# Weights' loads behind the squares' exchange, look-ups in front of the transposition, values' products in the squares' order

## The chip, the cores and the metric

The kernel runs on one core of one Trainium2 chip. The metric is the device time of one execution in microseconds; lower is better. A core has a matrix engine (TensorE, PE in the profile, with its weight loads as PEld), a vector engine (VectorE, DVE), a scalar engine (ScalarE, ACT), GpSimd (POOL) and SyncE (SP), which here only issues transfers. Each engine works through its own instructions in order; semaphores tie them together. Sixteen DMA engines move the data, and the transfers that one engine issues stand in one queue.

## The reference

Two transformer layers on `x` of 8 sequences x 512 tokens x 256 features, all in float32. Layer 0 is a rotating recurrence and a mixture of 16 experts. Layer 1 is causal attention with 16 heads of 128 and a feed-forward layer whose three weight matrices are looked up in a table of 16 values. The change lies in layer 1:

```python
# attention, W_K, W_Q, W_V: (16, 128, 256)
scores = jnp.einsum('biph,biqh->biqp', k, q)
masked = scores * mask - 1e10 * (1.0 - mask)
attn = softmax(masked / sqrt(128), axis=-1)
z = jnp.einsum('biqp,biph->biqh', attn, v)
out = jnp.einsum('df,bqf->bqd', W_O, z_flat)
# feed-forward, lut: (16,), *_idx: integers 0..15
h = silu(x @ lut[gate_idx].T) * (x @ lut[up_idx].T)
x = x + h @ lut[down_idx].T
```

## The kernel before

The span has four parts: layer 0 up to about 570 us, the attention of layer 1 from 570 to 2046 us, then the feed-forward layer to the end at 2277 us. The change is in the attention.

**The turns.** The attention is one Python loop over 8 sequences x 8 pairs of heads x 2 heads (`for p in range(ALL)`, `for e in range(2)`): 128 passes, called turns here. A turn is counted from its first score product, and numbered 0 to 15 in its sequence; sequences are numbered 0 to 7. Even turns have e = 0, odd turns e = 1. The order in which PE, DVE and SP are given their instructions is the order in which the loop calls them (`tc.manual_schedule(engines={ENG.PE, ENG.DVE, ENG.SP})`); ACT and POOL are ordered by a scheduler.

**One head passes through three turns.** In its first, `scores(0..3)` makes the four causal score tiles of 128 queries (PE, L1070), masks them and takes the extreme value (DVE, L1074), and exponentiates with the sum (ACT, L1085). `normalized` scales the tiles by the reciprocal sum (DVE L1093, ACT L1099) into `slots`, a tile of 10 blocks in 32-wide pieces. In the second turn the probabilities are transposed without TensorE: `squares_turned` transposes each 32 x 32 square (DVE, L1108) and writes the squares to memory with four transfers (SP, L1111); `exchanged` reads them back as `pT` in the order of the squares (SP, L1116), which completes the transposition of the whole. In the third turn `weigh` multiplies the values by `pT` (PE, L1140, four products into the PSUM bank `pz`) and copies the result to `z` (ACT, L1147). So a turn works on three heads: scores of one, exchange of the one before (`front`), values' products of the one before that (`rear`). `pT` and `pz` have one buffer each, `slots` two. The last two heads are turned by TensorE instead (`turned`, L1118).

**Projections.** Queries, keys, values and the output are made by a scheme of seven products in place of eight (`Sevens`, L239 to 264): four products and the sums on DVE in `first`, three products in `second`. Even turns make queries and the first half of keys for the next pair (`nxt`); odd turns finish the keys (`nxt.second(1)`) and make half of the values of the next group (`ahead`). The PSUM banks `pa` and `pb` are single, so the products of `ahead.second` wait until DVE has read `pb` (L253).

**Weights.** When a `second` has used a weight tile, `following_weights` loads the one for a later pair at once (`load_weights`, L739 to 745: 128 KB from the input and, once the five sums of the tile are kept in memory, 320 KB from there). The tiles `w0`, `w1` have two buffers, `wv` and `wo` one. The load waits for the last product that reads the old tile, and SP can issue nothing else while it waits.

**Outputs.** Every four heads, `Outputs` makes the products with the output weights (L1194) in four pieces, one in each turn at the call `one_out()`; a quarter's last piece also asks for the next `wo`. With the last quarter of a sequence GpSimd adds the kept sums (`summed`, L1210), and two more pieces turn the result with four transposes by TensorE each (L1229). In turns 2, 3 and 4 of a sequence a second `one_out()` stands in front of `scores(2)` where enough pieces are left.

**Look-ups.** The table look-ups for the feed-forward layer (`lookups`, L947 to 953) are spread over the attention: a generator, of which each turn from sequence 1 on takes one step on DVE, behind `weigh`.

Of the kernel before, what the change touches and what calls it, by code (L numbers as in the profile page):

```python
# [10 lines left out]
F32 = mybir.dt.float32  # L11
I32 = mybir.dt.int32
AF = mybir.ActivationFunctionType
# [102 lines left out]
def two_layers(ctx: ExitStack, tc: tile.TileContext, a: dict, out: bass.AP):  # L116
# [848 lines left out]
    with tc.tile_pool(name="big", bufs=2, side="right") as big, tc.tile_pool(  # L965
# [31 lines left out]
            return [pool.tile([P, T], F32, tag=tag, name=tag).rearrange("p (k t) -> p k t", k=2) for _ in range(2)]  # L997

        incomplete = []

        def following_weights(n, part):
            if part is not None:
                w, complete = load_weights(n, part, part not in seen_parts[n])
                weights[n].append(w)
                seen_parts[n].add(part)
                if complete:
                    incomplete.append((n, complete))
# [49 lines left out]
        class Head:  # L1057
# [29 lines left out]
            def normalized(self, *tiles):  # L1087

                if 0 in tiles:
                    self.slots = ap2.tile([P, NQ, NS, SQ], F32, name="slots")  # L1090
                w = self.slots
                rd = self.rd[:, tiles[0] : tiles[-1] + 1]
                nc.vector.reciprocal(rd, self.den[:, tiles[0] : tiles[-1] + 1])  # L1093
                for i in tiles:

                    for j in range(0, i + 1, 2):
                        n = min(i + 1 - j, 2)
                        at, step = SLOT[j, i], SLOT[j + n - 1, i] - SLOT[j, i]
                        nc.scalar.activation(  # L1099
                            w[:, :, at : at + step + 1 : max(step, 1), :].rearrange("p q j k -> p j q k"),  # L1100
                            self.pr[i][:, j * P : (j + n) * P].rearrange("p (j q k) -> p j q k", q=NQ, k=SQ),
                            AF.Copy,
                            scale=self.rd[:, i : i + 1],
                        )

            def squares_turned(self):

# [27 lines left out]

            def weigh(self):

                pz = pzp.tile([P, T], F32, tag="pz", name="pz")
                for j in range(NT):
                    nc.tensor.matmul(  # L1140
                        pz[:, j * P :].rearrange("p (i q k) -> p i q k", q=NQ, k=SQ),
                        self.v(j),
                        self.of_keys(j),
                        start=(j == 0),
                        stop=(j == NT - 1),
                    )
                nc.scalar.copy(self.z, pz)  # L1147


        late = []  # L1150
# [1 line left out]
        def in_time():  # L1152
            while late:
                late.pop(0)()
# [82 lines left out]
        def outputs(quarter, eng=nc.gpsimd):  # L1237

            quarter.combined(eng)
            last = quarter.q == NGRP - 1  # L1240
            n = quarter.b * NGRP + quarter.q + 1

            def end(*banks):
                quarter.products(3, *banks)
                if n < NB * NGRP:
                    following_weights("o", n % NGRP)
                if last:
                    in_time()
                    quarter.summed(eng)

            pieces = [lambda *banks, i=i: quarter.products(i, *banks) for i in range(3)] + [end]
            if last:
                pieces += [lambda *banks, h=h: quarter.turned(h, *banks) for h in range(2)]
            return pieces

        def one_out():
# [30 lines left out]
        with tc.manual_schedule(engines={ENG.PE, ENG.DVE, ENG.SP}):  # L1287
            seqs[0].xn = first_xn
            for c in range(NC):
                seqs[0].turned(c)  # L1290
            seqs[0].combined()
            following_weights("o", 0)

            pairs[0].first(0)
            pairs[0].first(1, lambda: other_banks(psc, "sc"))
            pairs[0].second(0, 2)
            groups[0].first(0)
            pairs[0].second(1, 2)
            groups[0].first(1, lambda: other_banks(ptp, "pt"))
            for s in range(2):  # L1300
                groups[0].second(s, s or None)

            front = rear = None
            for p in range(ALL):
                b, pair = divmod(p, NPAIR)
                nxt = pairs[p + 1] if p + 1 < ALL else None
                after = (p + 3) % NPAIR if p + 3 < ALL else None
                ahead = groups[p // 2 + 1] if p // 2 + 1 < len(groups) else None
                if pair % 2 == 0:
                    z = big.tile([P, VG, T], F32, tag="big", name="zT")  # L1310
                for e in range(2):
                    head = Head(
                        *(pairs[p].of_head(n, e) for n in range(2)),
                        lambda j, g=groups[p // 2], h=2 * (p % 2) + e: g.of_head(j, h),
                        z[:, 2 * (pair % 2) + e, :],
                        e,
                        p < ALL - 1,
                    )
                    in_time()
                    if front and not front.by_slots:  # L1320
                        one_out()
                        rear.weigh()
                        front.turned()
                        rear = None
                    head.scores(0)
                    head.scores(1)
                    if front and front.by_slots:
                        front.squares_turned()
                    one_out()
                    if nxt:  # L1330
                        nxt.second(1, after) if e else nxt.first(0)
                    if rear:
                        rear.weigh()
                    in_time()
                    while rows_to_gather and rows_to_gather[0][0] <= 2 * p + e:
                        gather(*rows_to_gather.pop(0)[1])
                    if b:
                        next(look, None)
                    if rear and e and pair % 2 == 0:
                        quarter = Outputs(*divmod(p // 2 - 1, NGRP), done, kept)  # L1340
                        tiles_out += outputs(quarter)
                    if not e and nxt:
                        nxt.second(0, after)
                    if e and ahead:
                        ahead.first(p % 2)
                    if head.by_slots:
                        head.normalized(0, 1)

                    slot = (2 * pair + e) % VG
                    if slot != 1 and len(tiles_out) > -slot % VG + 1:  # L1350
                        one_out()
                    head.scores(2)
                    head.scores(3)
                    if front and front.by_slots:
                        front.exchanged()
                    in_time()
                    if e and ahead:
                        last_half = p % 2 == 1
                        ahead.second(p % 2, (p // 2 + 2) % NGRP if last_half and p // 2 + 2 < len(groups) else None)
                    if not e and nxt:  # L1360
                        nxt.first(1)
                    if head.by_slots:
                        head.normalized(2)
                        head.normalized(3)

                    complete_weights(*(("v",), (0, 1, "o"))[e])
                    front, rear = head, front

                    if pair == 3 and e == 0 and b + 1 in together:
                        taken = row_stats(*together[b + 1])  # L1370
                        if len(together[b + 1]) > 1:
                            next(taken)
# [11 lines left out]
            one_out()  # L1384
            rear.weigh()
# [210 lines left out]
```

## Time and profile before

| | us |
|---|---|
| three runs | 2278.41, 2270.70, 2278.88 (median 2278.41) |
| profiled execution | 2278.94 |
| its span, first to last instruction | 2277.2 |
| attention stage (570 to 2046) | 1476 |
| TensorE busy, whole span | 2123.3 (93%) |
| VectorE busy, whole span | 1716.0 (75%) |
| ScalarE busy, whole span | 1181.6 (52%) |
| GpSimd busy, whole span | 428.1 (19%) |
| mean granted TensorE clock | 0.989 |

In a list of waits a line names the engine and line that waited, what it waited for, the total in us, the number of times and the longest. In a list of groups a line names the line, engine, operation, output and input, the shape and the count; then the busy time, the mean duration in ns and the idle time in front. In a timeline a line has the start (us from the span's start), the duration, the engine and the operation; in brackets stands the idle time before it and what ended it. A product in float32 stands as two matrix instructions.

### The profile page before, as it was taken

The numbers are of one execution on the slowest core, as the hardware profiler recorded it, in microseconds if no ns is written. First come the engines' busy times: TensorE is split into PE (matmuls) and PEld (weight loads), VectorE is DVE, ScalarE is ACT, GpSimd is POOL, SyncE is SP. The second block draws the span as 40 slices with busy tenths as digits, with TensorE's granted clock in tenths as the row PEclk, the third lists the DMA queues.
The fourth block names the chain that finished last, engine by engine and source line by source line (L and its number), as shares of the span: only waits on it lengthen the run. The fifth ranks groups of instructions, "written<-read, shape, count | busy, mean of one in ns | idle before, by whom it ended". The sixth has DMA issues, their size and how long they took to land. (4 is left out here: it accounts for less than half of the span.)

```text
span 2277.2 us, 29531 instructions
## 1 busy us (share of the span) xinstructions
PE 2123.3 (93%) x8733; PEld 1551.5 (68%) x8733; DVE 1716.0 (75%) x4269; ACT 1181.6 (52%) x2943; POOL 428.1 (19%) x438
## 2 busy tenths in 40 slices
PE   6999998998899999999999999988999999989999
PEld 3554545886577776777677777766776767658887
DVE  6788887555667778778777877888877887868765
ACT  5767761433565555555556555545555555643211
POOL 0022234002463312121221131121011111010000
PEclk9999999999999999999999999999999999999999
DMA  5111217652677766666757666765666675530000
GB/s 192 46 70 64 75 63 247 193 159 82 191 223 223 221 200 199 211 204 201 226 186 213 205 210 193 215 199 174 185 191 199 190 213 182 176 94 10 19 19 28
DMA packets 208640, 363.98 MB, mean 160 GB/s; under 512 B 27120, under 2 KB 145952, under 8 KB 208480
## 3 DMA queue, kind: packets, MB, share of 16 engines
q1 hardware_dynamic: 197712, 333.62, 47.5%
q0 software_dynamic: 8112, 25.31, 3.4%
q10 hardware_dynamic: 2656, 3.17, 0.4%
q8 instruction: 70, 1.15, 0.2%
q14 instruction: 90, 0.74, 0.1%
HBM read 241.29 MB, written 120.72 MB: 159 GB/s over the span
## 5 line engine op out<-in xcount | busy, mean ns | idle before, releaser
L1099 ACT ACTIVATE slots<-pr,rd 128x128 f32<-128x128 f32 x756 | 302.2, 463 | 236.2 <-DVE rd L1093 162.1
L1140 PE MATMUL pz<-pT,v 128*128 128x512 f32 (+3 forms) x1024 | 306.8, 443 | 30.1 <-DMA pT<-squares 29.7
L1070 PE MATMUL sc<-qk,qk 128*128 128x128 f32 (+3 forms) x1024 | 321.4, 437 | 4.6 <-DVE low L1074 4.5
L1085 ACT ACTIVATE pr<-ms,low 128x128 f32<-128x128 f32 (+3 forms) x512 | 282.0, 552 | 41.1 <-DVE low L1074 39.5
L1140 PEld LDWEIGHTS pz<-pT,v 128*128 128x128 f32 x1024 | 192.0, 192 | 158.7 <-issue 63.9
L1074 DVE CUSTOM_DVE_ANT_0 ms<-sc,mask 128x128 f32<-128x128 f32 (+3 forms) x512 | 235.8, 482 | 50.4 <-PE sc L1070 46.9
L1108 DVE STREAM_TRANSPOSE slots<-slots 128x1280 f32<-128x1280 f32 x126 | 190.2, 1510 | 102.0 <-ACT slots L1099 101.9
L1147 ACT COPY zT<-pz 128x512 f32<-128x512 f32 x128 | 74.9, 585 | 281.9 <-PE pz L1140 260.4
L239 PE MATMUL pb<-tT,w 128*128 128x256 f32 x762 | 208.8, 383 | 3.6 <-DVE qk L253 3.0
L1070 PEld LDWEIGHTS sc<-qk,qk 128*128 128x128 f32 x1024 | 174.9, 193 | 52.0 <-ACT slots L1099 5.3
L893 POOL DMA_INDIRECT yg<-ys,yrow x64 | 66.1, 1032 | 613.2 <-DVE x L900 452.8
L239 PEld LDWEIGHTS pb<-tT,w 128*128 128x128 f32 x762 | 140.2, 192 | 23.1 <-DVE qk L253 5.9
L239 PE MATMUL pa<-xT,w 128*128 128x256 f32 x508 | 151.6, 380 | 0.0
L239 PE MATMUL pb<-wv,tT 128*128 128x256 f32 x378 | 106.5, 390 | 39.9 <-DVE v L253 31.6
L632 POOL DMA_INDIRECT xs<-xn,slot x64 | 83.8, 1309 | 306.1 <-DVE share L642 122.8
L251 DVE TENSOR_TENSOR u<-pa,p 128x256 f32<-128x256 f32 x230 | 96.3, 419 | 50.3 <-ACT p L249 45.3
L239 PEld LDWEIGHTS pb<-wv,tT 128*128 128x128 f32 x378 | 68.2, 189 | 89.8 <-DVE v L253 65.3
L1194 PE MATMUL po<-zS,wo 128*128 128x256 f32 x512 | 125.9, 379 | 1.2 <-DVE kept L1205 1.2
L252 DVE TENSOR_TENSOR p<-pb,u 128x256 f32<-128x256 f32 x230 | 97.5, 424 | 25.1 <-PE pb L239 1.8
L262 DVE TENSOR_TENSOR qk<-pb,u 128x512 f32<-128x512 f32 x127 | 85.1, 670 | 38.0 <-PE pb L239 35.3
L1171 POOL TENSOR_TENSOR zS<-zT 128x512 f32<-128x512 f32 x31 | 40.4, 1302 | 372.8 <-PE po L1194 372.8
L1194 PEld LDWEIGHTS po<-zS,wo 128*128 128x128 f32 x512 | 97.2, 190 | 15.2 <-issue 2.1
(314 smaller groups left out, 4256.7 us busy)
## 6 DMA issues: line engine op xcount, KB each, us to landing
squares<-slots SPq DMA_DIRECT2D x504, 160.0 KB
pT<-squares SPq DMA_DIRECT2D x126, 640.0 KB
w<-sqk SPq DMA_DIRECT2D x112, 320.0 KB
w<-in_aqk SPq DMA_DIRECT2D x144, 128.0 KB
wv<-sv SPq DMA_DIRECT2D x28, 640.0 KB
wo<-so SPq DMA_DIRECT2D x28, 640.0 KB
xb<-xs SPq DMA_DIRECT2D x79, 128.0 KB
ys<-yb SPq DMA_DIRECT2D x79, 128.0 KB
```

The costliest lines, as they stand in the source:

```text
L239: nc.tensor.matmul(to, lhsT, rhs, start=first, stop=True, skip_group_check=True)
L251: nc.vector.tensor_tensor(self.u2, pa[:, 1, :], p1, ALU.add)
L252: nc.vector.tensor_tensor(p1, pb[:, 0, :], self.u2, ALU.add)
L262: nc.vector.tensor_tensor(self.out[:, :2, :], pb, self.u2.unsqueeze(1).to_broadcast([P, 2, HT]), ALU.add)
L632: nc.gpsimd.indirect_dma_start(out=xs, out_offset=bass.IndirectOffsetOnAxis(ap=slot[:, k, t : t + 1], axis=0), in_=self.xn[t], in_offset=None,
L1070: nc.tensor.matmul(sc[:, :kw], self.qT[:, i * P : kw], self.kT[:, :kw], start=True, stop=True)
L1074: nc.vector.tensor_tensor_reduce(out=ms[:, :kw], in0=sc[:, :kw], in1=mask[:, T - kw :], scale=-1.0 / math.sqrt(DH), scalar=3e38, op0=ALU.a ...
L1085: nc.scalar.activation(pr, ms[:, :kw], AF.Exp, bias=low, scale=-1.0, accum_out=self.den[:, i : i + 1])
L1099: nc.scalar.activation(w[:, :, at : at + step + 1 : max(step, 1), :].rearrange("p q j k -> p j q k"), self.pr[i][:, j * P : (j + n) * P].r ...
L1108: nc.vector.transpose(self.slots, self.slots)
L1140: nc.tensor.matmul(pz[:, j * P :].rearrange("p (i q k) -> p i q k", q=NQ, k=SQ), self.v(j), self.of_keys(j), start=(j == 0), stop=(j == NT ...
L1194: nc.tensor.matmul(po[:, m, :], self.w[:, n, k * P : (k + 1) * P], self.sides[n][:, k, :], start=(k == 0), stop=(k == 1),)
```

## The change

Four edits, all in the attention:

- `following_weights` only notes a load in a list. `load_following` issues what is noted: behind `exchanged`, behind `ahead.second`, after the setup, and at once where the load is one of `wo`. So the loads of `w0` and `w1` stand behind the `pT` load on SP.
- In odd turns the look-up's step is taken in front of `squares_turned` instead of behind `weigh`. In even turns it stays.
- Of a sequence's last quarter, the list of output pieces gets an empty piece in front of the two turning pieces, so in turn 4 the first turning piece is called by the second `one_out()`, in front of `scores(2)`.
- `pz` has the order of `pT` (32-wide squares outermost). The values' products read `pT` in runs of up to 128 elements and write `pz` in runs of 128, 96, 64 or 32; ScalarE's copy reads `pz` in the other order and writes `z` as before.

A branch that is never taken (`if False`) has been added around the scaling in `normalized`; the instructions are the same.

```diff
+        to_load = []
 
         def following_weights(n, part):
             if part is not None:
+                to_load.append((n, part))
+                if n == "o":
+                    load_following()
+
+        def load_following():
+            while to_load:
+                n, part = to_load.pop(0)
                 w, complete = load_weights(n, part, part not in seen_parts[n])
                 weights[n].append(w)
...
-                pz = pzp.tile([P, T], F32, tag="pz", name="pz")
+                pz = pzp.tile([P, NQ, NT, SQ], F32, tag="pz", name="pz")
                 for j in range(NT):
                     nc.tensor.matmul(
-                        pz[:, j * P :].rearrange("p (i q k) -> p i q k", q=NQ, k=SQ),
+                        pz[:, :, j:, :].rearrange("p q i k -> p q (i k)"),
                         self.v(j),
-                        self.of_keys(j),
+                        self.pT[:, :, SLOT[j, j] : SLOT[j, j] + NT - j, :].rearrange("p q i k -> p q (i k)"),
                         start=(j == 0),
                         stop=(j == NT - 1),
                     )
-                nc.scalar.copy(self.z, pz)
+                nc.scalar.copy(self.z.rearrange("p (i q k) -> p i q k", q=NQ, k=SQ), pz.rearrange("p q i k -> p i q k"))
...
-                pieces += [lambda *banks, h=h: quarter.turned(h, *banks) for h in range(2)]
+                pieces += [lambda *banks: None] + [lambda *banks, h=h: quarter.turned(h, *banks) for h in range(2)]
...
                     head.scores(0)
                     head.scores(1)
+                    if b and e:
+                        next(look, None)
                     if front and front.by_slots:
                         front.squares_turned()
                     one_out()
...
-                    if b:
+                    if b and not e:
                         next(look, None)
...
                     if front and front.by_slots:
                         front.exchanged()
+                    load_following()
                     in_time()
                     if e and ahead:
                         last_half = p % 2 == 1
                         ahead.second(p % 2, (p // 2 + 2) % NGRP if last_half and p // 2 + 2 < len(groups) else None)
+                    load_following()
```

More of the change, by code (lines that the diff above doesn't have):

```diff
@@ L1098, in normalized @@
                         at, step = SLOT[j, i], SLOT[j + n - 1, i] - SLOT[j, i]
[L1099 to L1104, printed above, removed]
+                        to = w[:, :, at : at + step + 1 : max(step, 1), :].rearrange("p q j k -> p j q k")
+                        pr = self.pr[i][:, j * P : (j + n) * P].rearrange("p (j q k) -> p j q k", q=NQ, k=SQ)
+                        rd = self.rd[:, i : i + 1]
+                        if False:
+                            nc.vector.tensor_scalar(to, pr, rd, None, ALU.mult)
+                        else:
+                            nc.scalar.activation(to, pr, AF.Copy, scale=rd)
             def squares_turned(self):
@@ L1355, in two_layers @@
                         front.exchanged()
+                    load_following()
                     in_time()
@@ L1359, in two_layers @@
                         ahead.second(p % 2, (p // 2 + 2) % NGRP if last_half and p // 2 + 2 < len(groups) else None)
+                    load_following()
                     if not e and nxt:
@@ L1384, in two_layers @@
             one_out()
+            load_following()
             rear.weigh()
```

## The prediction

> **What bounds the kernel now.** First the page's busy rows (first fence): TensorE is busy for 93% of the span and VectorE for 75%. Then the same per stretch: the attention stage (570 to 2046 us) holds 128 turns of 11.5 us, and TensorE leaves about 100 us of it idle. Only that idle time can be won. The DMA row stays at 6 to 7 tenths there, so transfers have room, and what counts is when each lands.
>
> ```profile
> PE 2123.3 (93%) x8733; PEld 1551.5 (68%) x8733; DVE 1716.0 (75%) x4269; ACT 1181.6 (52%) x2943; POOL 428.1 (19%) x438
> DMA  5111217652677766666757666765666675530000
> ```
>
> Next, who ended TensorE's idle time in that stage, and then what SyncE's queue and VectorE's transposition waited for:
>
> ```profile
> PE pb L239 <- DVE v L253: 31.6, 19, 3.6
> PE pz L1140 <- DMA pT<-squares: 29.7, 33, 2.7
> PE po L1229 <- POOL kept L1210: 10.3, 7, 2.7
> PE po L1194 <- DMA wo<-in_ao: 4.3, 5, 1.8
> ...
> SPq L739 <- PE pa L239: 146.4, 78, 5.9
> SPq L1116 <- DMA squares<-slots: 55.3, 62, 2.3
> ...
> DVE slots L1108 <- ACT slots L1099: 101.9, 101, 1.1
> ```
>
> Three waits of TensorE (v, pT, kept) make 71.6 us, and the change touches each. The queue waits for TensorE (L739) with the pT load standing behind it. The transposition waits 1 us in 101 turns of 126.
>
> The timeline shows two places that decide what can be won. Sequence 3, the end of turn 3 and turn 4 (which begins at 1156.4):
>
> ```profile
> 1151.91 0.71 SPq L739 DMA_DIRECT2D w<-in_aqk  x1
> 1153.78 0.33 SPq L739 DMA_DIRECT2D wo<-in_ao  x1
> 1154.75 0.32 SPq L1116 DMA_DIRECT2D pT<-squares  x1
> 1159.16 0.55 PE L1229 MATMUL po<-ident,kept 128*128 128x128 f32 x3 [1.85 <-POOL kept L1210]
> 1162.31 2.42 PE L1140 MATMUL pz<-pT,v 128*128 128x512 f32 x8 [0.87 <-DMA pT<-squares]
> ```
>
> TensorE waits for GpSimd, and right after it again for pT, which was issued behind w and wo. The second place is turn 1 (begun at 1121.3) and the start of turn 2:
>
> ```profile
> 1124.26 1.51 DVE L1108 STREAM_TRANSPOSE slots<-slots 128x1280 f32<-128x1280 f32 x1 [1.06 <-ACT slots L1099]
> ...
> 1127.72 0.70 SPq L739 DMA_DIRECT2D wo<-in_ao  x1
> ...
> 1132.34 1.99 PE L1194 MATMUL po<-zT,wo 128*128 128x256 f32 x8 [0.67 <-DMA wo<-in_ao]
> ```
>
> In turns 1, 9 and 13 the next wo follows the squares in SyncE's order, and turn 2, 10 or 14 begins with products of it. Over the timeline wo's first part lands about 6.2 us after the transposition ends, so a later transposition starts those products later.
>
> **The change, part by part.** The sum is made against the profiled execution, 2278.94 us (span 2277.2); it lies 0.5 us above the median of the runs shown. No instruction is added: the moves are of order.
>
> *Weights behind the exchange.* In all 126 exchanged turns but 7, pT leaves SyncE before the two loads of w (448 KB) instead of after. Issue: the mean is 9.56 us into a turn; the last square lands at 8.4 to 9.4, so some 0.5 us earlier. Landing: 5.07 us after issue in the middle, 4.1 in the fastest tenth, which I take as pT without w ahead: 1.0 us. So 1.5 us earlier per turn, at most 2.4 where SyncE waited longest. Who is passed: w only. It lands some 3 us later, and is multiplied two turns on, 23 us; the cover is large (in sequence 0 GpSimd's sums of a new w stand between, 2.3 us, still covered). v's load kept its place; wo still passes ahead of pT in turns 1, 9, 13, and in turn 3, where its issue empties the list of loads first, w is ahead too.
>
> *Look-up in front of the transposition* (odd turns, sequences 1 to 7, 56 turns). A look-up costs 607 + 966 = 1573 ns in sequences 1 to 4 and 2 x (455 + 615) = 2140 ns in 5 to 7, from these rows:
>
> ```profile
> L953 DVE TENSOR_TENSOR fs<-fs,tmp 128x688 f32<-128x688 f32 x60 | 58.0, 966 | 2.1
> L953 DVE TENSOR_TENSOR fd<-fd,tmp 128x256 f32<-128x256 f32 x75 | 46.1, 615 | 2.6
> L950 DVE TENSOR_SCALAR tmp<-idx,lut 128x688 f32<-128x688 int32 x60 | 36.4, 607 | 0.0
> L950 DVE TENSOR_SCALAR tmp<-idx,lut 128x256 f32<-128x256 int32 x75 | 34.1, 455 | 1.2
> ```
>
> The idle time that it can fill is 1.06 us in turns 1, 3, 5, 11 and 15, half of that on average in 7 and 9 (none where row statistics stand before), none in 13 (backlog after the token sums of turn 12): mean 0.8. So VectorE reaches v (L253) up to 1.06 us earlier, and the transposition ends later by 0.5 / 1.1 us (sequences 1 to 4 / 5 to 7) in the first group and 1.6 / 2.1 us in turn 13. Behind it stand qk (L262), the four squares, wo, pT.
>
> *An empty piece before the turned outputs.* The transposes (4 x 0.11 = 0.43 us) move in turn 4 from before to after the values' products, and GpSimd's sums are done by then: the 10.3 us wait goes. Late next is pT: it lands 16.1 to 17.1 us after turn 3 began, while TensorE would then be ready at 13.6 to 13.9. The addition to x (L1233, 0.67 us on VectorE) moves with it behind the fourth score tile, where turn 4 has idle time. It waits 2.5 to 3.3 us instead of twice, and still has 0.43 us to do.
>
> *Products in the squares' order.* Same columns; the operand is read in longer runs, and three of four products write PSUM in runs of 96, 64, 32. Reading in runs of 32 costs nothing today: 492 ns for 384 columns against 486 for the contiguous score product. No row shows a strided PSUM write. ScalarE's 384-wide copy into runs of 32 takes 479 ns, 11 ns above the straight line between its contiguous 256 (351) and 512 (585) copies, so I take 0. Ends: a gain of 6 ns x 8 x 126 = 6 us if the reads matter after all; if the strided columns (768 x 2 passes at 0.84 ns) took twice as long, +163 us. ScalarE's copy of pz (585 ns) reads in runs; twice as long would be +74 us on an engine that idles 260 us before that very copy.
>
> [...]
>
> Sum by pairs of turns, since an odd turn's DMA chain ends in the next one (us over all sequences):
> - sequence 0, no look-ups: four waits for pT over 1 us lose 1.25 each: -5.
> - 1 to 2: turn 1's waits (v 0.98, pT 0.43 a sequence) go, but turn 2 starts with wo, landing at 4.45 + 0.5 + 6.2 = 11.2 (11.8 later); its values' products follow 3.46 us later, at 14.7 (15.3), against 15.0 to 15.7 now, 19.1 in sequence 5: -4.
> - 3 to 4: the empty piece trades its wait for pT; +0.43 in six sequences, -2 in sequence 1, and 0.3 x 7 from the later squares: +3.
> - 5 to 6 (no wo): v 1.24 and pT 0.39 mostly go, limited by the look-up's 1.06: -6.5.
> - 7 to 8: pT lands later by 0.7 to 1.2 where statistics stand before, four sequences: +2.
> - 9 to 10: v's gain is eaten by wo: 0. 11 to 12: nothing waits: 0.
> - 13 to 14: no idle time to fill, wo's products start 0.3 to 0.8 us later: +3.
> - 15 to 0: -2.5.
>
> Together -10: 2278.9 - 10 = 2269 us. Bounds: if none of the delays reached TensorE, the five gains alone (-5 - 4 - 6.5 - 2.5, and -2) are -20; if the look-up gave nothing and its delay all passed in turns 3, 7 and 13, about +5. So 2259 to 2284 for this case.
>
> A clock row bears on turn 4. After a wait of 3.13 us the granted clock fell to 0.67 for 4 us (1734 to 1738), 1.7 us lost; after waits of 2.9 us in the timeline it fell in one case and not in another. I take 0; one drop in every sequence would be +12. [...]
>
> **The rivals.**
> - *The gains add up.* For: each wait is named in the profile. Against: turn 4 and wo. Two thirds of pT's 29.7 us and v's 14 us more: 34 us less, 2245.
> - *The later transposition decides* (slower). Place: odd turns 1, 3, 7, 9, 13, 35 turns. Price: mean look-up 1.8 less 0.8 us of idle = 1.0 us each, 35 us, less the 20 of gains: +15, 2294. It decides once the slack between wo's or pT's landing and its use, 0.0 to 0.6 us in turns 1 and 9 today, is below the delay. For: wo's four waits sit there. Against: pT loses w.
> - *Nothing moves.* The loads stay hidden and every wait is replaced by the next: 2278.
>
> **How the numbers follow.** Forecast 0.45, gains add up 0.22, slower 0.22, nothing 0.11. About 0.5% (11 us) is what a measurement can tell from no change. Faster: 0.17 of the forecast, all of the second, 0.01 of the last = 0.40. Slower: 0.20 of the third, 0.01 of the forecast = 0.21. The rest, 0.39, is the same. Range 2240 to 2294: it leaves out half of the second and half of the third case's spread, and a slow PSUM write (0.02).
>
> **What would show it.** Right: TensorE's wait for pT falls from 29.7 to some 20, gathered in turn 4; the wait for kept (L1210's sums) is gone; v's falls from 31.6 by a third; wo's rises from 4.3 to 10 or more; the transposition's idle time falls from 101.9 to about 55. Wrong: pz products longer than 2.16 us for eight, wo's wait unchanged, or the granted clock low in turn 4.

## The result and the profile after

The changed kernel takes 2297.29 us (median of four runs, 2297.17 to 2299.03), the kernel before 2278.40 beside it: a ratio of 1.0093, 95% interval 1.0071 to 1.0115. It is slower by 19 us going by the medians (21 by the ratio), where 2269 was forecast. The profiled execution has a span of 2295.4 us, 18.2 more than before.

The busy row, from the page of the changed kernel:

```profile
PE 2131.9 (93%) x8733; PEld 1557.8 (68%) x8733; DVE 1700.0 (74%) x4269; ACT 1183.4 (52%) x2943; POOL 415.8 (18%) x438
```

The instructions are the same in number. VectorE is busy 16 us less. TensorE is busy 9 us more on the same products, a sign of the clock: the mean granted clock is 0.984 (0.989 before). Then the waits of the changed kernel in the attention stage, for TensorE, SyncE's queue and the transposition:

```profile
PE pz L1150 <- DMA pT<-squares: 47.9, 41, 3.5
PE po L1204 <- DMA wo<-in_ao: 22.3, 20, 3.1
PE pb L239 <- DVE qk L262: 21.5, 18, 2.3
...
PE pb L239 <- DVE qk L253: 7.9, 11, 2.4
...
SPq L1126 <- DMA squares<-slots: 290.8, 195, 4.9
...
SPq L739 <- PE pa L239: 23.5, 35, 5.3
...
DVE slots L1118 <- ACT slots L1114: 59.6, 60, 1.1
```

The waits for v (31.6 us) and for the kept sums (10.3) have gone, as the edits intended. In their place TensorE waits 47.9 us for pT (29.7 before), 22.3 for wo (4.3) and 21.5 for qk (8.1). SyncE's wait for TensorE (L739) fell from 146.4 to 23.5 us, and its wait for the squares, in front of the pT load, rose from 55.3 to 290.8.

The two places of the prediction, in the timeline of the changed kernel. Turn 1 of sequence 3, begun at 1133.7:

```profile
1135.46 0.57 DVE L950 TENSOR_SCALAR tmp<-idx,lut 128x688 f32<-128x688 int32 x1
1135.52 1.65 POOL L1181 TENSOR_TENSOR zS<-zT 128x512 f32<-128x512 f32 x1 [4.94 <-PE po L1204]
1136.07 1.83 DVE L953 TENSOR_TENSOR fs<-fs,tmp 128x688 f32<-128x688 f32 x1
...
1137.82 1.50 DVE L1118 STREAM_TRANSPOSE slots<-slots 128x1280 f32<-128x1280 f32 x1
...
1139.35 1.88 SPq L1121 DMA_DIRECT2D squares<-slots  x4
1141.27 0.71 SPq L739 DMA_DIRECT2D wo<-in_ao  x1
...
1145.80 1.56 PE L1204 MATMUL po<-zT,wo 128*128 128x256 f32 x6 [1.27 <-DMA wo<-in_ao]
```

The look-up now stands in front of the transposition, and its addition takes 1.83 us, beside a GpSimd sum (L1181). The transposition ends 5.6 us into the turn instead of 4.5, wo is issued behind the squares 1.2 us later in the turn than before, and its first product waits at the start of turn 2. And the end of turn 3 with turn 4, begun at 1169.7:

```profile
1165.49 0.70 SPq L739 DMA_DIRECT2D w<-in_aqk  x1
...
1167.12 0.33 SPq L739 DMA_DIRECT2D wo<-in_ao  x1
...
1168.12 0.32 SPq L1126 DMA_DIRECT2D pT<-squares  x1
...
1174.50 2.42 PE L1150 MATMUL pz<-pT,v 128*128 128x512 f32 x8 [2.02 <-DMA pT<-squares]
```

w and wo still go ahead of pT here, and the one wait that is left is for pT.

Where the time came from, by pairs of turns (lengths of turns from one score product to the next, us over all sequences, after less before):

| pair | predicted | changed kernel |
|---|---|---|
| sequence 0 | -5 | +6.2 |
| 1-2 | -4 | +6.3 |
| 3-4 | +3 | +10.4 |
| 5-6 | -6.5 | -9.1 |
| 7-8 | +2 | -0.1 |
| 9-10 | 0 | +2.3 |
| 11-12 | 0 | 0.0 |
| 13-14 | +3 | +6.9 |
| 15-0 | -2.5 | -3.0 |
| sum | -10 | +19.9 |

The stage also starts 2.2 us earlier. A pair's figure compares two single traces: with the order of the products alone changed (d_order below), which costs nothing, single pairs still read -4.2 to +4.6. So differences under about 5 us in one pair say little.

One more sum goes across all pairs: TensorE's time at half clock (a granted clock of 0.5) in the attention stage is 58.0 us (30.7 before). A values' product of 512 columns took 1.06 us at half clock in the changed kernel, 0.59 otherwise. If up to half of that time is lost (an estimate from these), it is 29.0 against 15.4 us: a difference of up to 13.7 beside the 18.2 us by which the span grew.

Three theories stand for the loss. *Late transposition*: the look-ups delay the squares and with them wo and pT. *Clock*: short waits, merged into long ones, let the clock fall. *Order of the loads or of the products*: one of these costs by itself.

### The profile page after: what moved, and what is told of

Its sections match the earlier page's. It is cut to its first block, busy times and chain, and to the rows that moved or that the text cites. A ratio compares the mean times of both kernels' runs of the same rounds, so it can differ in the third digit from the quotient of the medians.

```text
span 2295.4 us, 29596 instructions
## 1 busy us (share of the span) xinstructions
PE 2131.9 (93%) x8733; PEld 1557.8 (68%) x8733; DVE 1700.0 (74%) x4269; ACT 1183.4 (52%) x2943; POOL 415.8 (18%) x438
## 3 DMA queue, kind: packets, MB, share of 16 engines
q8 instruction: 70, 1.15, 0.2%
## 4 chain that ended last, share of the span: by engine, by line
PE 49%; DMA 10%; DVE 9%; issue 2%; ACT 1%; SPq 1%; DVEq 0%; ACTq 0%
PE pb L239 12%; PE pz L1150 10%; PE pa L239 9%; PE sc L1079 8%; DMA pT<-squares 8%; PE po L1204 5%; PE py L1472 4%; DVE slots L1118 2%; DMA squares<-slots 1%; DVE ms L1083 1%; DMA wo<-in_ao 1%; SPq L1121 1%; DVE p L252 1%; DVE u L251 1%; PE pm L190 1%
## 5 line engine op out<-in xcount | busy, mean ns | idle before, releaser
L1150 PE MATMUL pz<-pT,v 128*128 128x512 f32 (+3 forms) x1024 | 312.2, 449 | 48.9 <-DMA pT<-squares 47.9
L1079 PE MATMUL sc<-qk,qk 128*128 128x128 f32 (+3 forms) x1024 | 326.4, 442 | 2.6 <-DVE low L1083 2.6
L1118 DVE STREAM_TRANSPOSE slots<-slots 128x1280 f32<-128x1280 f32 x126 | 189.9, 1508 | 59.8 <-ACT slots L1114 59.6
L239 PEld LDWEIGHTS pb<-tT,w 128*128 128x128 f32 x762 | 139.9, 191 | 27.7 <-DVE qk L253 10.9
L239 PE MATMUL pb<-wv,tT 128*128 128x256 f32 x378 | 105.8, 389 | 21.5 <-DVE qk L262 21.5
L1204 PE MATMUL po<-zT,wo 128*128 128x256 f32 x384 | 98.7, 395 | 22.3 <-DMA wo<-in_ao 22.3
```

Of the source, the lines that this page charges most:

```text
L239: nc.tensor.matmul(to, lhsT, rhs, start=first, stop=True, skip_group_check=True)
L1079: nc.tensor.matmul(sc[:, :kw], self.qT[:, i * P : kw], self.kT[:, :kw], start=True, stop=True)
L1118: nc.vector.transpose(self.slots, self.slots)
L1150: nc.tensor.matmul(pz[:, :, j:, :].rearrange("p q i k -> p q (i k)"), self.v(j), self.pT[:, :, SLOT[j, j] : SLOT[j, j] + NT - j, :].rearra ...
L1204: nc.tensor.matmul(po[:, m, :], self.w[:, n, k * P : (k + 1) * P], self.sides[n][:, k, :], start=(k == 0), stop=(k == 1),)
```

## Experiments

All ratios are against the kernel before, run on the same chip.

| kernel | median us | ratio | 95% interval |
|---|---|---|---|
| changed kernel | 2297.29 | 1.0093 | 1.0071 to 1.0115 |
| a_loads: loads alone | 2277.63 | 0.9975 | 0.9958 to 0.9991 |
| b_look: look-ups alone | 2304.61 | 1.0077 | 1.0058 to 1.0095 |
| c_piece: empty piece alone | 2296.18 | 1.0061 | 1.0040 to 1.0081 |
| d_order: products' order alone | 2283.45 | 0.9996 | 0.9977 to 1.0016 |
| look_late | 2271.02 | 0.9970 | 0.9950 to 0.9990 |
| busy4 | 2283.38 | 1.0020 | 1.0002 to 1.0038 |
| wo_ahead | 2251.81 | 0.9898 | 0.9881 to 0.9915 |
| best5 | 2258.91 | 0.9912 | 0.9890 to 0.9934 |
| best5c | 2263.45 | 0.9933 | 0.9912 to 0.9954 |
| best6 | 2251.11 | 0.9884 | 0.9866 to 0.9902 |
| best7 | 2245.06 | 0.9848 | 0.9825 to 0.9871 |
| all_moves | 2203.52 | 0.9665 | 0.9642 to 0.9689 |

### The four parts, each alone

Each is the kernel before with one edit of the change. a_loads:

```diff
         def following_weights(n, part):
             if part is not None:
+                to_load.append((n, part))
+                if n == "o":
+                    load_following()
```

> The kernel before with the first edit alone: the loads of w0 and w1 behind the load of pT. The late-transposition theory (the loss of the change as a whole comes from the look-ups that delay the transposition, and from clock drops after the one long wait in turn 4) expects a gain here: pT lands about 1 us earlier in the turns of even pairs, and the 29.7 us of waits for pT shrink by about half, so 2278 - 15 = 2263 us (2258 to 2270). The loads theory (pT now waits behind the squares, and w, issued late, stands in front of the next turn's squares) expects no gain or a loss: 2278 to 2290.

b_look:

```diff
+                    if b and e:
+                        next(look, None)
                     if front and front.by_slots:
                         front.squares_turned()
...
-                    if b:
+                    if b and not e:
                         next(look, None)
```

> The kernel before with the second edit alone: the look-up of odd turns in front of the transposition. The late-transposition theory expects most of the loss here: the transposition of turns 1, 3, 9 and 13 ends 0.5 to 1.5 us later, w still passes ahead of pT, so TensorE waits longer for wo in turn 2, 10, 14 and for pT in turn 4, 8: +15 to +30 us, 2293 to 2308. Its rival (the look-up fills VectorE's idle time, and the waits for v, 31.6 us, go) expects 2265 to 2272.

c_piece:

```diff
-                pieces += [lambda *banks, h=h: quarter.turned(h, *banks) for h in range(2)]
+                pieces += [lambda *banks: None] + [lambda *banks, h=h: quarter.turned(h, *banks) for h in range(2)]
```

> The kernel before with the third edit alone: the empty piece in front of the turned outputs. By the trace of the changed kernel the wait for the kept sums (10.3 us) goes, and pT, landing at the same time as before, takes its place as a single wait of about 3 us in turn 4. The clock theory expects the granted clock low for 3.4 us after it in most of the seven sequences, 1.7 us lost each: +5 to +15 us, 2283 to 2293. Its rival (the clock drops of the changed kernel come from elsewhere) expects -2 to +3, 2276 to 2281, with the clock of turn 4 as before.

d_order:

```diff
-                        pz[:, j * P :].rearrange("p (i q k) -> p i q k", q=NQ, k=SQ),
+                        pz[:, :, j:, :].rearrange("p q i k -> p q (i k)"),
...
-                        self.of_keys(j),
+                        self.pT[:, :, SLOT[j, j] : SLOT[j, j] + NT - j, :].rearrange("p q i k -> p q (i k)"),
```

> The kernel before with the fourth edit alone: values' products in the squares' order. Both the late-transposition theory and the clock theory expect 2278 +- 4 us: the eight instructions of the products take 3.55 us in the changed kernel as before (449 and 443 ns each), and ScalarE's copy 585 ns in both. A theory that the strided PSUM writes cost something unseen in the groups expects +5 us or more.

Measured: -0.25%, +0.77%, +0.61% and -0.04%, together +1.09%, within the interval of the whole (+0.71 to +1.15%). Two of the parts make the loss. That the total agrees is in part chance: by the medians the four make +1.6%, and pair by pair they do not add up (5-6: +5.1, -5.1, +7.2 and +0.4 alone, -9.1 together). The order of the products costs nothing that these runs resolve: the middle duration is the same for each of the four widths before and with this edit (592, 486, 379 and 275 ns). The mean in the changed kernel's groups (449 ns, 443 before) has the lower clock in it; ScalarE's copy takes 585 ns in both:

```profile
L1150 PE MATMUL pz<-pT,v 128*128 128x512 f32 (+3 forms) x1024 | 312.2, 449 | 48.9 <-DMA pT<-squares 47.9
...
L1157 ACT COPY zT<-pz 128x512 f32<-128x512 f32 x128 | 74.9, 585 | 289.9 <-PE pz L1150 270.5
```

The loads bring 5.7 us by the ratio, a gain, but a third of what the first theory expected. pT's waits fell to 23.0 us, not by half, and the waits for v rose from 31.6 to 38.6.

The look-ups alone lose 17.6 us by the ratio (23.1 by the medians), within the +15 to +30 that the late transposition expected, and lose where it said. By pairs: 1-2 +8.1, 9-10 +8.1, 13-14 +9.7, with gains at 5-6 (-5.1) and 15-0 (-2.2).

The empty piece alone loses 14 us, but only half of it in turn 4 (+7.8). The clock was low there in three of seven sequences (one before), less than "most". The waits of that turn grew by 3.8 us and its half-clock time from 3.4 to 10.2 us, 3.4 us lost by the same estimate: 7.2 of the 7.8. Its waits in the list of c_piece:

```profile
PE pz L1149 <- DMA pT<-squares: 42.4, 39, 3.2
PE pb L239 <- DVE v L253: 30.1, 21, 3.1
```

pT's wait grew by 12.7 us, more than the 10.3 us of the kept sums that it replaced. The pair 5-6 lost 7.2 us more, for a reason that no theory had: turn 5's look-up, behind the values' products, now ran into GpSimd's sum, and its addition took 1.82 us instead of 0.88 in sequences 2 to 4, where turn 5 grew from about 10.0 to 11.1 us. In sequence 2 the addition starts 6.49 us into the turn and a sum of GpSimd at 6.09; before, the addition came first (6.14 against 6.58). In a_loads the same happened (1.83 us in sequences 2 to 4, where the turn took 10.75 us; 0.88 in sequence 1, where it took 10.19).

### Look-ups back behind the products, in five of eight odd turns (look_late)

```diff
-                    if b and e:
+                    front_look = 2 * pair + e in {11, 5, 15}
+                    if b and front_look:
                         next(look, None)
...
-                    if b and not e:
+                    if b and not front_look:
                         next(look, None)
```

> The changed kernel with the look-up in front of the transposition only in turns 5, 11 and 15; in turns 1, 3, 7, 9 and 13 it stands behind the values' products again. The late-transposition theory (the look-up delays the squares, and so wo and pT, by more than the idle time it fills in exactly these five) expects the losses of the pairs 1-2 (+6.3 us against the kernel before), 9-10 (+2.3) and 13-14 (+6.9) to go, and of 3-4 (+10.4) some 3: 2297 - 15 to 20 = 2277 to 2282 us; TensorE's waits for wo fall from 22.3 to below 8 us. Its rival (the loss is the clock's and comes with any order that leaves one long wait) expects 2290 or more.

Measured 2271.02 us, faster than expected. Waits for wo fell from 22.3 to 7.8 us. By pairs: 1-2 from +6.3 to -2.8, 9-10 from +2.3 to -6.7, 13-14 from +6.9 to -0.8; 3-4 stayed at +10.9, where some 3 us less had been expected. Putting the look-up back behind the products in those turns makes a loss of 0.93% a gain of 0.30%. So the look-ups in front carry most of the loss, in three of the five turns. Pair 3-4 is not its work.

### wo ahead of the squares (wo_ahead)

```diff
+                    one_out()
                     if front and front.by_slots:
                         front.squares_turned()
-                    one_out()
```

> The changed kernel with the output piece called before the transposition, so that in turns 1, 9 and 13 the next wo stands in front of the squares in SyncE's order and does not wait for them. If the late transposition costs its time through wo (TensorE waits 22.3 us for it, 20 times), these waits fall below 8 us and the time falls by some 12 to 16 us, to 2281 to 2285 us. If it costs it through pT (the squares now stand behind wo, and pT lands late all the same), waits for wo become waits for pT of turns 2, 10 and 14 and the time stays at 2293 to 2300 us.

All look-ups stay in front here. Measured 2251.81 us, a gain twice as large as the theory expected. TensorE's first line of waits is now pT, and no wait for wo is left:

```profile
PE pz L1150 <- DMA pT<-squares: 40.0, 26, 3.8
PE pb L239 <- DVE qk L262: 23.1, 18, 2.3
```

The timeline of wo_ahead, the same turn 1 of sequence 3 (begun at 1112.65):

```profile
1114.36 0.33 SPq L739 DMA_DIRECT2D wo<-in_ao  x1
...
1115.05 1.83 DVE L953 TENSOR_TENSOR fs<-fs,tmp 128x688 f32<-128x688 f32 x1
...
1116.80 1.50 DVE L1118 STREAM_TRANSPOSE slots<-slots 128x1280 f32<-128x1280 f32 x1
...
1118.33 1.95 SPq L1121 DMA_DIRECT2D squares<-slots  x4
...
1123.74 1.89 PE L1204 MATMUL po<-zT,wo 128*128 128x256 f32 x8
```

The addition is as slow and the transposition as late as in the changed kernel, but wo leaves 1.7 us into the turn instead of 7.6, and its product waits for nothing. Against the changed kernel the pairs 1-2, 9-10, 13-14 and sequence 0 gain 13.9, 13.3, 9.7 and 8.8 us. So the path of the loss is the place of wo on SyncE's queue, behind the squares, with pT behind both. Means of sequences 1 to 7, in us into the turn (a load's landing is read from its semaphore; a product that waits for it starts 0.04 us later):

| | before | changed kernel | wo_ahead |
|---|---|---|---|
| wo issued, turn 1 | 6.6 | 7.8 | 1.8 |
| wo issued, turn 9 | 7.8 | 9.1 | 1.7 |
| wo issued, turn 13 | 7.8 | 9.3 | 1.7 |
| pT lands, turn 1 | 15.4 | 16.5 | 14.7 |
| pT lands, turn 9 | 16.8 | 17.6 | 15.7 |
| pT lands, turn 13 | 16.5 | 17.9 | 16.0 |

In these turns pT lands later in the changed kernel than before, though w no longer goes ahead of it. The spans of the changed kernel and wo_ahead differ by 48.3 us: 22.3 are the waits for wo, 7.9 those for pT, and up to 12.0 half of the time at half clock (58.0 to 34.1 us). The expectation had priced the waits alone. In the attention stage of the two traces the order of instructions is the same on TensorE and ScalarE and, but for two instructions moved by a few places in sequence 7, on VectorE. GpSimd's order differs in a few places of the first two sequences. So SyncE's queue is nearly the only thing moved.

### TensorE kept at work in turn 4 (busy4)

```diff
                     if rear:
+                        if b and 2 * pair + e == 4:
+                            idle = pzp.tile([P, NQ, NT, SQ], F32, tag="pz", name="pz")
+                            for _ in range(12):
+                                nc.tensor.matmul(idle[:, 0], ident, ident, start=True, stop=True)
                         rear.weigh()
```

> The changed kernel with 12 spare products of 128 x 128 (their result is not used) in front of the values' products in turn 4 of the sequences 1 to 7, where TensorE waits some 3 us for pT, so that it works while it waits. The clock theory (five of the seven waits of turn 4 are followed by 3.4 to 6.8 us at half clock, 1.7 to 3.4 us lost each) expects no half clock within turn 4 and 2297 - 10 = 2287 us (2285 to 2290). If the wait alone counts, and not the clock, the time stays at 2297 or grows by as much as the spare products (12 x 2 x 0.11 = 2.6 us a sequence) outlast the wait: 2296 to 2302.

Adding work made it faster: a ratio of 1.0020 against 1.0093, intervals apart. The windows from 4 to 11 us into turn 4, sequences 1 to 7 (window, length, busy time and instructions of each engine; then the granted clock, the DMA share and GB/s), of the changed kernel:

```profile
801.80:808.80 7.00, 5.95 (x19) 4.32 (x20) 3.45 (x8) 1.05 (x3) 0.98 (x1) 0.76 0.79 270
989.90:996.90 7.00, 5.47 (x17) 3.72 (x18) 3.16 (x7) 0.62 (x2) 1.06 (x1) 0.76 0.73 245
1173.70:1180.70 7.00, 6.20 (x26) 4.38 (x27) 4.53 (x11) 2.47 (x6) 1.06 (x1) 1.00 0.75 258
1358.30:1365.30 7.00, 4.77 (x12) 2.97 (x13) 2.63 (x6) 0.59 (x1) 1.06 (x1) 0.76 0.72 275
1543.40:1550.40 7.00, 4.79 (x9) 2.95 (x10) 3.17 (x9) 0.11 (x1) 0.00 (x0) 0.61 0.64 246
1731.30:1738.30 7.00, 6.30 (x20) 4.32 (x21) 3.12 (x9) 1.40 (x4) 0.00 (x0) 0.76 0.72 246
1913.20:1920.20 7.00, 5.05 (x21) 3.57 (x22) 3.40 (x10) 1.76 (x4) 0.00 (x0) 1.00 0.64 233
```

and the first two of busy4 (the other five show 1.00 too):

```profile
808.20:815.20 7.00, 6.57 (x36) 4.91 (x35) 3.75 (x9) 1.76 (x4) 0.97 (x1) 1.00 0.69 259
993.30:1000.30 7.00, 5.49 (x32) 4.33 (x32) 3.43 (x8) 0.91 (x2) 1.06 (x1) 1.00 0.72 276
```

The clock was low in five of seven, and in none with the spare products: the drop is the idle time's. How much it is worth is less sharp. The two ratios differ by 0.7%, some 16 us; in the profiled execution, the longest of this kernel's runs, turn 4 alone is at +7.2 us instead of +12.8.

### What is left when the losing parts go (best5, best5c, best6, best7, all_moves)

best5 is the kernel look_late without the empty piece:

```diff
-                pieces += [lambda *banks: None] + [lambda *banks, h=h: quarter.turned(h, *banks) for h in range(2)]
+                pieces += [lambda *banks, h=h: quarter.turned(h, *banks) for h in range(2)]
```

> The same, and the empty piece taken out as well: the loads behind the exchange, the look-up in front in turns 5, 11 and 15 alone, and the products in the squares' order. If the parts add up as they did alone (loads -0.25%, order 0, empty piece +0.6% of which half sits in turn 5), it should beat the kernel before: the loads' 5 us and the waits for v in turn 5 (some 8 us), 2278 - 13 = 2265 us (2260 to 2270). A rival (each wait that goes is replaced by the next, so only the loads' 5 us stay) expects 2272 to 2276.

Measured 2258.91, beyond the hopeful end by a little; the empty piece costs 0.58% here (0.9970 against 0.9912) and 0.61% alone. Pair 5-6 gains 12.7 us, 3-4 loses 1.9.

best5c is look_late with the last quarter's next wo noted like the others:

```diff
-        def following_weights(n, part):
+        def following_weights(n, part, at_once=True):
...
-                if n == "o":
+                if n == "o" and at_once:
                     load_following()
...
-                    following_weights("o", n % NGRP)
+                    following_weights("o", n % NGRP, not last)
```

> The kernel with the look-up in front in turns 5, 11 and 15 alone, with the empty piece, and with the load of the last quarter's next wo noted like those of w0 and w1, so that in turn 3 nothing of w or wo passes ahead of pT. If the empty piece costs only because pT of turn 3 lands late (16.6 us after the turn began, TensorE ready at 13.9), pT should land about 1 to 1.5 us earlier, the wait of turn 4 should fall from 3.5 to about 2 us, the clock should stay at full speed, and the time should be 8 to 12 us below that with the empty piece and wo ahead of pT. If pT lands late because its squares are late, the time stays the same within 3 us.

The time is 0.37% (8 us) below look_late, at the near end of what was expected, but not for a shorter wait alone: TensorE's wait for pT in turn 4 fell from 2.5 to 0.1 us a sequence, and a new one of 1.7 us stood in turn 5, since wo now went ahead of the next pT. (These are the waits for pT alone; the next expectation puts the loss at 3.65 and 2.62 us.) Pair 3-4 went to -12.7 us and 5-6 from -10.5 to +5.8.

best6 holds that wo back until turn 4's pT has been issued:

```diff
                         front.exchanged()
+                    if 2 * pair + e == 4:
+                        to_load[:0] = wo_later
+                        wo_later.clear()
                     load_following()
```

> The look-up in front in turns 5, 11 and 15 alone, with the empty piece, and the load of the last quarter's next wo held back to turn 4, behind its pT. With it behind the exchange of turn 3 the wait for pT went from turn 4 (3.65 us a sequence) to turn 5 (2.62 us), because wo then stood ahead of the next pT. If the place of wo on the queue is the cause, turn 4 stays short (pair 3-4 some 13 us below the kernel before) and turn 5 is short again (pair 5-6 some 11 us below): 2263 - 15 = 2248 us (2243 to 2253). If wo collides with whatever stands behind it, the wait moves on to a later turn and the time stays at 2260 to 2266 us.

Measured 2251.11, inside: 3-4 at -12.7 and 5-6 at -9.6. With nothing ahead of pT the pair 3-4 with the empty piece is 12.7 us below the kernel before, where the piece alone lost 7.8 us. What the piece itself brings here is open: no run holds wo back without it.

best7 takes three look-ups of odd turns in even turns:

```diff
-                    if b and not front_look:
+                    if b and not front_look and 2 * pair + e not in {1, 9, 13}:
                         next(look, None)
+                        if 2 * pair + e in {2, 8, 12}:
+                            next(look, None)
```

> The same, and the look-ups of turns 1, 9 and 13, where VectorE is late for v (1.0, 1.2 and 3.0 us a sequence), are taken in turns 2, 8 and 12 in addition to theirs, where VectorE idles 4.0, 2.4 and 1.9 us. If VectorE's work in the turn sets the wait for v, the waits for v (26 us) go and 15 to 25 us are won: 2225 to 2235 us. If they are replaced by the next wait (pT of the following turn), or the doubled look-up delays the even turns, the time stays at 2243 to 2253 us.

Measured 2245.06: the rival, for the most part. The waits for v went (24.7 to 1.4 us), but those for pT grew from 20.5 to 27.5 and for wo from 5.6 to 14.2. The waits of best7, and below them those of all_moves, which adds the edit of wo_ahead to it:

```profile
PE pz L1154 <- DMA pT<-squares: 27.5, 29, 2.5
PE po L1208 <- DMA wo<-in_ao: 14.2, 15, 3.1
```

> The kernel with the look-ups of turns 1, 9 and 13 taken in turns 2, 8 and 12 and with the last quarter's wo held back to turn 4, and now with the output piece in front of the transposition too, so that the other loads of wo do not wait for the squares. If the waits of 14.2 us for wo that are left in it are the queue's, as they were in the changed kernel, they go, and the time falls by 14 to 25 us: 2245 - 20 = 2225 us (2218 to 2232). If pT, which then stands behind wo, takes their place in turns 2, 10 and 14, the time stays at 2238 to 2248 us.

```profile
PE pz L1154 <- DMA pT<-squares: 12.8, 14, 3.9
...
PE pb L239 <- DVE qk L253: 9.4, 24, 2.1
PE pb L239 <- DVE qk L262: 8.9, 12, 1.1
```

Measured 2203.52 us, 3.35% below the kernel before: twice the expected step. Waits for wo fell by 14.2 us and for pT by 14.7, and half of the drop in half-clock time (30.7 to 6.8 us) is 12.0: 41 of the 45.5 us between the spans. It is the fastest kernel of this study. Every edit of the change is in it, but the look-ups stand in front of the transposition in turns 5, 11 and 15 alone, and each load of wo has another place on SyncE's queue.

## Why the prediction was wrong

The direction was wrong, and the time lay 3 us above the range. The rival "the later transposition decides" had the direction and most of the place, at a chance of 0.22. That its price (2294) came so near is in part luck: the pairs 1-2, 7-8, 9-10 and 13-14 made +15 us, and 17 more came from the pair 3-4 and sequence 0, which are not its work.

- **Weights behind the exchange.** "Landing 1.0 us earlier" came out at 0.9 (5.0 to 4.1 us after issue in the middle). "Issue 0.5 us earlier" did not: with this edit alone 0.3 us earlier, in the changed kernel 0.2 later (9.6 to 9.8 us into a turn), because in odd turns the squares come later and pT waits for them. Together pT lands 0.3 us earlier in the turn on average, not 1.5, and later by 0.8 to 1.5 us in turns 1, 9 and 13 (the table at wo_ahead). Alone the edit gains 5.7 us.
- **Look-up in front of the transposition.** This step failed first. The sum let pT's gain of 1.5 us outweigh the later transposition in turns 1, 9 and 13. There wo and pT stand behind the squares, so both inherited the delay. Turn 2 was to gain because its values' products would follow wo with pT already there; its waits for wo rose from 0.9 to 6.8 us and those for pT from 2.6 to 5.6. So "1 to 2: -4" became +6.3, "9 to 10: 0" +2.3 (no more than the scatter), "13 to 14: +3" +6.9. The delay itself was also mis-sized, as its price was a mean (966 ns for the 128x688 addition). "0.5 / 1.1 us" for the first group measured 1.2 / 1.6 in turn 1, but 0.25 / 0.4 to 0.7 in turns 3, 11 and 15. The row of the kernel before with shortest, middle and longest shows what the mean mixes:

```profile
L953 DVE TENSOR_TENSOR fs<-fs,tmp x60: 874/876/1823, 764.6 to 1467.7; 128x688 f32<-128x688 f32 x60
```

  It takes 0.88 us, and 1.3 or 1.8 where a GpSimd sum is already running when it starts. These collisions sat in turns 3 and 13 before and moved to turn 1 and, in two sequences, turn 9. Of the prediction's signs, wo's wait ("from 4.3 to 10 or more") came out at 22.3 us, and the transposition's idle time (55) at 59.6.
- **Waits for v** did more than fall by a third: none is left. Part of them came back as waits for qk (8.1 to 21.5 us), which the sum had only named as standing behind the transposition.
- **Empty piece.** The exchange of kept for pT was right (3 us in one piece). The 0.43 us per sequence was too little: alone it costs 1.1 us a sequence in turn 4, half of that through the clock, and 7.2 us in all in the pair 5-6. "Turn 4 has idle time" was true, but the moved addition to x now stands at its very end, and VectorE's look-up of turn 5 comes 0.35 us later and runs into GpSimd's sum. In the change as a whole the look-up stands in front of turn 5's transposition, and 5-6 is at -9.1.
- **Clock.** "I take 0; one drop in every sequence would be +12" should have been near the +12. In turn 4 five of seven sequences dropped, and its time at half clock went from 3.4 to 20.5 us, 8.5 us more lost by the estimate of half. With 4.3 us more of waits (14.8 to 19.1) that makes 12.8, the growth of turn 4.
- **Sequence 0.** -5 became +6.2, the largest miss of the table. It has no look-ups and no empty piece. The waits for pT that were to go stayed (5.7 to 5.1 us). Turn 10 grew by 6.0 us, and a_loads alone shows 4.6 of them; the three other parts alone show at most 0.4. The loads of w do it through GpSimd, which in this sequence still makes the sums of each new w. The prediction had called these sums "still covered", and asked only when w is multiplied. As w lands later, they move back from 8.0 to 2.1 us ahead of turn 10's start, and GpSimd's next sums run on into that turn without a gap. VectorE's scaling of the rows (L175) then stands beside them, before and after:

```profile
679.24 1.97 DVE L175 TENSOR_SCALAR xnt<-x,st,rs 128x256 f32<-128x256 f32 x4
...
681.30 0.73 POOL L201 TENSOR_TENSOR wo<-wo 128x256 f32<-128x256 f32 x1 [1.22 <-DMA wo<-in_ao]
```

```profile
675.43 8.06 DVE L175 TENSOR_SCALAR xnt<-x,st,rs 128x256 f32<-128x256 f32 x4
...
679.38 0.72 POOL L201 TENSOR_TENSOR wo<-wo 128x256 f32<-128x256 f32 x1
```

  The first of the four instructions takes 6.2 us instead of 1.0, so the projections' sums on VectorE come late, and TensorE waits 2.4 us for qk and 1.3 for pT in that turn, which it did not before. Every kernel with the loads behind the exchange has these 8 us and a turn 10 longer by 4.2 to 7.2 us, but for wo_ahead and all_moves: there GpSimd's order is another, the scaling takes 4.7 and 4.4 us, and the turn is 0.9 and 0.6 longer. Most of turn 14's +2.0 is a half-clock stretch that b_look and d_order show too.
- **Products' order.** Right at 0. Writes in runs of 96, 64 and 32 took the same time (middle durations of 486, 379 and 275 ns, before and with the edit), so the "slow PSUM write (0.02)" of the range stands in no run. The 6 ns between 492 and 486 were the low clock's share of a mean: the middle duration is 486 ns for both. The sign "products longer than 2.16 us for eight" could not tell: the timeline has 2.42 us before and after.

## What to carry to other kernels

A queue's order decides what an edit on another engine costs: a load that stood behind transfers with a late source (wo behind the squares, issued 7.8 us into turn 1 instead of 1.8) inherited their lateness, and moving it ahead was worth twice its visible waits (48.3 us of the span against 22.3). Price an operation by its shortest and longest case (0.87 and 1.82 us for the 128x688 addition before) and by what runs beside it where it will stand, not by its mean. A load that lands later also moves the work of the engine that reads it, here GpSimd's sums, and that work can collide with an engine that the edit never touched (VectorE's scaling, 6.2 us instead of 1.0). Merging two short waits of TensorE into one long one is not neutral: half clock followed 99 of the 160 gaps of 2 us and more in the table below.

## What the runs showed of the hardware

**Which waits half clock followed.** Over the attention stage of all fourteen traces, TensorE's idle gaps of over 1 us, and how many had a half-clock stretch begin between 1.2 us before and 1.6 us after their end (a stretch counts for one gap):

| gap us | followed | of |
|---|---|---|
| 1.0 to 1.5 | 0 | 206 |
| 1.5 to 2.0 | 9 | 98 |
| 2.0 to 2.5 | 42 | 75 |
| 2.5 to 3.0 | 32 | 49 |
| 3.0 and over | 25 | 36 |

Of 110 half-clock stretches 108 belong to such a gap. They last 3.4 us or multiples of it (3.41, 6.83 and 10.24 us in the changed kernel). One followed more than half of the gaps of 2.0 to 2.5 us. That the gap is the cause was tried in turn 4 alone (busy4: no sequence of seven dropped, five in the changed kernel). The prediction had costed the waits by their length alone.

**VectorE beside GpSimd.** The 128x688 addition stands 60 times in each of the fourteen traces, 840 times in all:

| at its start | times | us |
|---|---|---|
| no GpSimd sum until its end | 674 | 0.874 to 0.878 |
| none, but one starts during it | 64 | 0.874 to 0.877 |
| one is running | 102 | 1.28 to 1.91 |

In the second row it is GpSimd's sum that grows, from 1.27 us to as much as 1.99. In the third row the addition ends 0.73 us after the running sum does, within 0.01 us each time. So an addition that starts first is not delayed (0.874 to 0.877 us), and 0.4 us decide, as in turn 5 of c_piece. The running sum need not be at its own 1.27 us: in the changed kernel it took 1.37 to 1.65, with the look-up's first instruction (L950) still running at its start. In the timeline above GpSimd's sum ends 1.1 us after the addition's start; 1.1 + 0.73 = 1.83 us, as measured. What makes the one wait for the other was not tried by itself.
